# Softplus as one ScalarE function, expert ranks from comparisons and running sums, and a lead-in in another order

## The chip, the core and the metric

The kernel runs on one core of a Trainium2 chip. The time is the device time of one execution in microseconds, as the median of several runs. TensorE (PE) multiplies matrices, VectorE (DVE), ScalarE (ACT) and GpSimd (POOL) work elementwise on 128 partitions, and SyncE (SP) issues transfers.

## The reference, cut to what matters

Four batches of 1024 tokens with 256 features pass through four residual blocks: a selective state-space block, a mixture of 512 tiny experts beside a dense MLP, a linear attention, and the same mixture again. All arithmetic is fp32.

```python
# state-space block on the layer-normed x
conv  = conv_b + sum(xp[:, k:k+L, :] * conv_w[:, k] for k in range(4))
x     = silu(conv)                                   # 512 channels
delta = softplus(x @ wd1.T @ wd2.T + wd2_b)
A     = -exp(A_log)                                  # 512 x 16
h     = exp(delta*A) * h + (delta*x) * B_l           # per token, 16 states
y     = einsum('ben,bn->be', h, C_l) + x * W_D
out   = resid + (y * silu(skip)) @ out_w.T

# experts: two queries per token against 64 keys each
scores2, idx2 = top_k(routing, 8)                    # sx, sy and ix, iy
all_scores = sx[:, :, None] + sy[:, None, :]         # 64 pairs
all_idx    = ix[:, :, None] * 64 + iy[:, None, :]
scores, pk = top_k(all_scores, 8)
indices    = all_idx[pk]                             # beyond 511: the gather takes 511
ew  = silu(x @ down_embed[indices]) * softmax(scores)
out = ew @ up_embed[indices] + (silu(x @ gate_w) * (x @ up_w)) @ down_w
```

## The kernel before

The 4096 tokens are eight groups of 512; two groups are one sequence. Four stages follow one another.

**Scan.** For each group and each of the 16 states there is one step `s`, cut into two halves of two 128-channel tiles. In a half GpSimd multiplies `u = dx * bt` (`times_b`, L717; `bt` is a row of B, read back from DRAM to all partitions), ScalarE computes two decays `a = exp(delta * a_neg)` (`decay`, L731), DVE runs two recurrences `h` of 512 tokens, TensorE transposes the last step's `h`, and DVE adds it, times C, onto `acc` (`sum_up`). Beside this, work of other groups is woven in by generators: `prepare` makes the next group's projections, convolution, `delta` and `dx`; `finish` and `norm` end the last group; `mlp` is the dense MLP of earlier groups. Each `yield` in them names an estimated cost for TensorE and ScalarE, and `tick` (L640), called once per half step, decides by these costs which stages go out. A stage whose ScalarE cost exceeds `LONG = 4.0` is a lump: a table load, a function over 128x2048, and a load back for the decays. The engine orders come out pinned as written.

`softplus(z)` was built from pieces (`parts`, L362, to `chain`, L424): `e = |z|` and `delta = relu(z)` on ScalarE, `e = exp(-e)`, `dx = e + 1`, `delta += e` on GpSimd, `e = ln(dx)`, `dx -= 1`, `delta -= dx`, `delta += e`; then `dx = delta * xc`. In the first group (`alone`), DVE does the elementwise part.

**Lead-in** (L674 to L704). Ahead of the first step: GpSimd scales the identity into convolution taps `cds` and `w_d`, then `statistics(0)`, `prepare(0)`, the stores of `conv_d`, loads of x, and `a_neg`; `statistics(1)` comes at the first step (L769).

**Experts** (`experts`, L1155). For each group `route` (L977) makes a table `tb` of the weights of the 512 experts, per token: the top 8 of each query's 64 scores (`max`, `max_index`), the pairs' top 8, and with `iota`-comparisons a threshold `most` for each of the eight x-keys and a `rank` for each of the 64 y-keys; GpSimd multiplies out all 8 x 64 weights, and DVE sets those with a rank over the threshold to zero. A 128x2048 `eq` buffer serves both. `route` is a generator too, advanced one stage in each of eight steps per group. TensorE transposes `tb` into PSUM, which `apply` multiplies onto `wt`; the rest of the MLP queue runs beside it.

**Attention**, and then **ffn** (L1337), the last block: per group sixteen gate and up products, the experts, `route(g + 1)`, and `raise_x`.

Of the kernel before, what the change touches and what calls it, by code (L numbers as in the profile page):

```python
# [13 lines left out]
U32 = mybir.dt.uint32  # L14
# [6 lines left out]
P = 128  # L21
# [30 lines left out]
class Net:  # L52
# [59 lines left out]
    def ssm(self, xs, hs, behind):  # L112
# [6 lines left out]
        with ExitStack() as ctx:  # L119
# [22 lines left out]
            def load_x(g):  # L142
                xw_at[g] = now[0]
                xw[g] = late4.tile([P, TG, D], F32, tag="x", name="xw")
                sp.dma_start(out=xw[g], in_=xv[g])
# [7 lines left out]
            in_w0 = weights("in_wT")  # L153
            conv_w = self.load(wp, "conv_w", [P, EC, KC])
# [11 lines left out]
            ones = wp.tile([P, 1], F32, tag="ones", name="ones")  # L166
            dve.memset(ones, 1.0)
            mones = wp.tile([P, 1], F32, tag="mones", name="mones")
            dve.memset(mones, -1.0)
# [76 lines left out]
            def prepare(g, got, cds=None):  # L246
# [7 lines left out]
                def evac(out, ps, scale=None, bias=None):  # L254
                    if not alone:
# [100 lines left out]


                delta = two.tile([P, EC, G], F32, tag="delta", name="delta")
                dx = two.tile([P, EC, G], F32, tag="dx", name="dx")
                e = one.tile([P, EC, G], F32, tag="xe", name="e")  # L360

                def parts(c, ps):  # L362
                    b = wd2_b[:, c : c + 1]
                    act.activation(e[:, c, :], ps, AF.Abs, bias=b)
                    if alone:
                        dve.tensor_scalar(delta[:, c, :], ps, b, 0.0, ALU.add, ALU.max)
                    else:
                        act.activation(delta[:, c, :], ps, AF.Relu, bias=b)

                ps = z(0)  # L370
                for c in range(EC - 1):
                    yield 0.9, 1.2
                    parts(c, ps)
                    ps = z(c + 1)
                yield 3.4, 1.2
                parts(EC - 1, ps)
                ps = bank([2 * N, G], "bc")
                mul(ps, [(wbc[:, c, :], xc[:, c, :]) for c in range(EC)])
                yield 0, 1.9
                act.activation(e, e, AF.Exp, scale=-1.0)  # L380
                yield 0.3, 2.6
# [10 lines left out]

                if alone:
                    dve.tensor_scalar(dx, e, 1.0, None, ALU.add)
                else:
                    act.activation(dx, e, AF.Identity, bias=ones)

                def tt(out, a, b, op, c):
                    elem.tensor_tensor(out[:, c, :], a[:, c, :], b[:, c, :], op)

                tt(delta, delta, e, ALU.add, 0)
                tt(delta, delta, e, ALU.add, 1)
                yield 0, 4.7
                cT = late2.tile([P, TG, N], F32, tag="cT", name="cT")
                evac(cT, ps[:, :, N:])
                tt(delta, delta, e, ALU.add, 2)
                tt(delta, delta, e, ALU.add, 3)
                act.activation(e, dx, AF.Ln)
                yield 1.7, 2
                if alone:  # L410
                    dve.tensor_scalar(dx, dx, -1.0, None, ALU.add)
                else:
                    act.activation(dx, dx, AF.Identity, bias=mones)
# [10 lines left out]
                def chain(c):  # L424
                    tt(delta, delta, dx, ALU.subtract, c)
                    tt(delta, delta, e, ALU.add, c)
                    tt(dx, delta, xc, ALU.mult, c)

                if alone:
                    for c in range(EC):  # L430
                        chain(c)
                ps = w_skip(0)
                for t in range(1, TG):
                    yield 1.7, 1.3
                    evac(gate[:, t - 1, :], ps)
                    ps = w_skip(t)
                    if not alone:
                        chain(t - 1)
# [15 lines left out]
                yield 0.9, 1.3  # L454
                evac(gate[:, TG - 1, :], ps)
                gates[g] = gate
                if not alone:
                    chain(TG - 1)
# [215 lines left out]
            with ExitStack() as lead:  # L674
                tp = lead.enter_context(tc.tile_pool(name="ssm_lead", bufs=1))
                cds = {}
                for c in range(EC):
                    cds[c] = tp.tile([P, KC, P], F32, tag=f"cd{c}", name=f"cd{c}")
                    for k in range(KC):
                        pool.tensor_scalar(  # L680
                            cds[c][:, k, :], self.ident, conv_w[:, c, k : k + 1], 1.0,
                            ALU.mult, ALU.mult,
                        )
                for c in range(EC):
                    pool.tensor_scalar(
                        w_d[:, c, :], self.ident, w_d_col[:, c : c + 1], 1.0,
                        ALU.mult, ALU.mult,
                    )
                for _ in statistics(0):
                    pass  # L690
                for _ in prepare(0, data[0], cds):
                    pass
                for c in range(EC):
                    sp.dma_start(out=conv_d[c], in_=cds[c])
                for g in range(1, 4):
                    load_x(g)
                act.activation(a_neg, a_log, AF.Exp)
                dve.tensor_scalar(a_neg, a_neg, -1.0, None, ALU.mult)
            thr = scan.enter_context(
                tc.tile_pool(name="ssm_thr", bufs=2, reuse_waits="tile")  # L700
            )
            four = scan.enter_context(
                tc.tile_pool(name="ssm_four", bufs=4, reuse_waits="tile")
            )  # L704
# [52 lines left out]
            for q in range(AHEAD):  # L757
                times_b(q)
            before, kept_state, stats, begun = None, None, iter(()), {0, 1}
            for s in range(NG * N):  # L760
                g, n = s // N, s % N
                first = g % 2 == 0
                if n == 0 and g + 1 < NG:
# [5 lines left out]
                    if g == 0:  # L769
                        for _ in statistics(1):  # L770
                            pass
# [177 lines left out]
    def expert_weights(self, pool):  # L949
        nc, w, eng = self.nc, {}, self.nc.sync  # L950
        w["W_q"] = self.load_rows(pool, "W_q", KD, 2 * NKEY, eng)

        w["keys"] = []
        for t in range(2):
            kb = pool.tile([P, 2, NKEY], F32, tag=f"keys{t}", name=f"keys{t}")
            nc.gpsimd.memset(kb, 0.0)
            for i in range(2):
                eng.dma_start(out=kb[i * 64 : (i + 1) * 64, i, :], in_=self.io["keys"][t])
            w["keys"].append(kb.rearrange("p a b -> p (a b)"))

        w["iota"] = pool.tile([P, NKEY], F32, tag="iota", name="iota")
        nc.gpsimd.iota(
            w["iota"], pattern=[[1, NKEY]], base=0, channel_multiplier=0,
            allow_small_or_imprecise_dtypes=True,
        )
        w["iota32"] = pool.tile([P, NKEY], F32, tag="iota32", name="iota32")
        nc.vector.tensor_scalar(w["iota32"], w["iota"], 32.0, None, ALU.mult)
        w["steps"] = pool.tile([P, TOPK], F32, tag="steps", name="steps")
        nc.vector.tensor_scalar(w["steps"], w["iota"][:, 0:TOPK], 1.0, None, ALU.add)
# [7 lines left out]
    def route(self, nc, w, g, qT, pools, got):  # L977
# [7 lines left out]
        M4 = 4  # L985
# [10 lines left out]
        r = sm.tile([P, 2 * M4, NKEY], F32, tag="r", name="r")  # L996
        nc.scalar.copy(r, ps.rearrange("p t m (h k) -> p (t m h) k", h=2))
        yield
        v = sm.tile([P, 2 * M4, TOPK], F32, tag="v", name="v")
        iu = sm.tile([P, 2 * M4, TOPK], U32, tag="iu", name="iu")  # L1000
        for i in range(2 * M4):
            if i == M4:
                yield
            nc.vector.max(v[:, i, :], r[:, i, :])
            nc.vector.max_index(iu[:, i, :], v[:, i, :], r[:, i, :])
        yield
        fi = sm.tile([P, 2 * M4, TOPK], F32, tag="fi", name="fi")
        nc.vector.tensor_copy(fi, iu)
        fx, fy = fi[:, 0:M4, :], fi[:, M4:, :]
# [3 lines left out]
        nc.vector.tensor_tensor(  # L1013
            d[:, :, :NKEY], r, top.to_broadcast([P, 2 * M4, NKEY]), ALU.subtract
        )
        nc.vector.tensor_tensor(
# [14 lines left out]

        pv, left, pw = pairs("pv"), pairs("left"), pairs("pw")
        nc.vector.tensor_tensor(
            grid(pv), over(v[:, 0:M4, :], 3), over(v[:, M4:, :], 2), ALU.add
        )
        sc = sm.tile([P, M4, TOPK], F32, tag="sc", name="sc")
        for i in range(M4):
            nc.vector.max(sc[:, i, :], pv[:, i, :])
            nc.vector.match_replace(left[:, i, :], sc[:, i, :], pv[:, i, :], -3.0e38)
        yield  # L1040
        nc.vector.tensor_tensor(left, left, pv, ALU.not_equal)
        cnt = sm.tile([P, M4, TOPK], F32, tag="cnt", name="cnt")
        nc.vector.tensor_reduce(cnt, grid(left), AX.X, ALU.add)

        nc.vector.tensor_tensor(
            grid(pw), over(d[:, 0:M4, NKEY:], 3), over(d[:, M4:, NKEY:], 2), ALU.mult
        )
        nc.vector.tensor_tensor(pw, pw, left, ALU.mult)
        zi = sm.tile([P, M4], F32, tag="zi", name="zi")
        nc.vector.tensor_reduce(zi, pw, AX.X, ALU.add)  # L1050
        nc.vector.reciprocal(zi, zi)

        f64 = sm.tile([P, M4, TOPK], F32, tag="f64", name="f64")
        nc.vector.tensor_scalar(f64, fx, float(NKEY), None, ALU.mult)
        nc.vector.tensor_tensor(grid(pv), over(f64, 3), over(fy, 2), ALU.add)
        nc.vector.scalar_tensor_tensor(
            pv, pv, float(NEXP - 1), pw, ALU.is_ge, ALU.mult
        )
        last = sm.tile([P, M4], F32, tag="last", name="last")
        nc.vector.tensor_reduce(last, pv, AX.X, ALU.add)  # L1060
        nc.vector.tensor_tensor(last, last, zi, ALU.mult)
        yield

        nc.vector.tensor_tensor(
            grid(pw), w["iota"][:, 0:TOPK].unsqueeze(1).unsqueeze(3).to_broadcast(sh),
            over(fx, 2), ALU.is_equal,
        )
# [389 lines left out]
```

## Time and profile before

| | |
|---|---|
| time, median of 3 runs | 2168.31 us (2165.47 to 2179.81) |
| the profiled execution | 2167.88 us, its span 2166.2 |
| granted TensorE clock | 0.955 |
| busy: TensorE, VectorE, ScalarE, GpSimd | 1914.2, 1592.9, 1019.4, 1032.6 us |
| chain that ended last, by engine | PE 57%, DVE 22%, ACT 12%, issue 5%, POOL 3%, DMA 2% |
| first recurrence, its second pair | 83.57 us, 91.10 us |
| scan, experts, attention, ffn | to about 1197, 1460, 1690, 2166 us |

Busy time is summed over the whole span; what bounds a stage is read from that stage. The chain that ended last is followed back from the last instruction, at each step to what released it. In a line for a group of instructions stand its line, engine and operation, output and inputs, shapes, count; then busy us and mean ns of one; then the engine's idle time just before. In a line for one tile, the three durations are minimum, median and maximum in ns.

### The profile page before, as it was taken

The page shows a single profiled execution, that of the slowest core. Times are in us where ns is not written, and L with a number is a line of the kernel's source. Part 1 is how long each engine was busy: PE and PEld are TensorE (multiplying, and loading weights), DVE is VectorE, ACT ScalarE, POOL GpSimd, SP SyncE. Part 2 cuts the span into 40 slices and gives each one's busy share as a digit, 9 for nine tenths or more (in the row PEclk, how much of TensorE's full clock was granted, in tenths as well). Part 3 has the DMA queues.
Part 4 walks back from the last instruction along what each step waited for, and adds up shares of the span by engine and source line. Part 5 has one row for each costly group of instructions (what it writes and reads, how often), then busy time and mean ns, then how long its engine had stood idle before and what let it go on. Part 6 is the DMA issues. An engine that isn't in the chain of part 4 may idle for free.

```text
span 2166.2 us, 22802 instructions
## 1 busy us (share of the span) xinstructions
PE 1914.2 (88%) x7712; PEld 1209.5 (56%) x7712; DVE 1592.9 (74%) x2843; ACT 1019.4 (47%) x1557; POOL 1032.6 (48%) x691
## 2 busy tenths in 40 slices
PE   6585888988979989899888889969998999999999
PEld 2334545655645655556464555646665456666665
DVE  2798998978989979888798789984446545555551
ACT  2366676767766777677656233213332311111111
POOL 2569779687787886877886223311111000000000
PEclk9798999999999999999999999989999999999999
DMA  2311212122122221221212222120000000000000
GB/s 74 98 54 27 81 49 76 51 79 76 52 83 73 72 73 52 76 81 50 73 40 88 98 77 89 49 83 1 1 1 1 1 10 10 10 10 10 10 10 10
DMA packets 84757, 106.13 MB, mean 49 GB/s; under 512 B 7840, under 2 KB 53920, under 8 KB 84640
## 3 DMA queue, kind: packets, MB, share of 16 engines
q1 hardware_dynamic: 78064, 98.00, 14.6%
q10 hardware_dynamic: 6576, 6.67, 1.0%
q8 instruction: 61, 1.00, 0.2%
q14 instruction: 56, 0.46, 0.1%
HBM read 90.75 MB, written 13.89 MB: 48 GB/s over the span
## 4 chain that ended last, share of the span: by engine, by line
PE 57%; DVE 22%; ACT 12%; issue 5%; POOL 3%; DMA 2%; ACTq 0%; SPq 0%; DVEq 0%; POOLq 0%
PE ps L106 23%; PE hT L47 5%; PE gate L47 4%; DVE h L47 4%; PE conv L47 4%; DVE acc L47 4%; PE up L47 3%; ACT L47 3%; ACT a L47 3%; PE xin L47 2%; PE dt L47 2%; PE out L47 2%; PE down L47 2%; DVE eq L47 1%; ACT av L47 1%
## 5 line engine op out<-in xcount | busy, mean ns | idle before, releaser
L47 POOL TENSOR_TENSOR u<-dx,bt 128x1024 f32<-128x1024 f32 x256 | 604.1, 2368 | 264.0 <-DVE h L47 137.0
L47 PE MATMUL hT<-ident,h 128*128 128x128 f32 x2048 | 305.7, 290 | 120.4 <-DVE acc L47 118.2
L47 DVE SCALAR_TENSOR_TENSOR acc<-hT,cT,acc 128x512 f32<-128x512 f32 x512 | 355.9, 736 | 40.3 <-PE hT L47 39.3
L47 PEld LDWEIGHTS hT<-ident,h 128*128 128x128 f32 x2048 | 247.2, 148 | 245.1 <-DVE acc L47 194.4
L47 ACT ACTIVATE a<-delta,a_neg 128x512 f32<-128x512 f32 x512 | 340.1, 688 | 92.1 <-DVE h L47 72.2
L47 DVE TENSOR_TENSOR_SCAN h<-a,state,u 128x512 f32<-128x512 f32 x256 | 314.9, 1267 | 38.7 <-ACT a L47 37.6
L47 DVE TENSOR_TENSOR_SCAN h<-a,u 128x512 f32<-128x512 f32 x256 | 299.4, 1206 | 59.2 <-ACT a L47 52.0
L1079 POOL TENSOR_TENSOR tb<-ex,d 128x2048 f32<-128x2048 f32 x8 | 29.2, 3644 | 400.7 <-PE ps L106 330.7
L1379 DVE TENSOR_TENSOR act<-s,ps 128x512 f32<-128x512 f32 x64 | 43.8, 685 | 145.2 <-PE ps L106 145.1
L1377 ACT ACTIVATE s<-ps 128x512 f32<-128x512 f32 x64 | 38.2, 597 | 230.1 <-PE ps L106 222.2
L47 ACT ACT_TABLE_LOAD x92 | 118.0, 1283 | 56.6 <-DVE d L47 33.9
L47 PE MATMUL gate<-hT,gate_w 128*128 128x512 f32 x256 | 124.2, 618 | 8.2 <-DMA gate_w<-in_gate_w 8.2
L47 PE MATMUL up<-hT,up_w 128*128 128x512 f32 x256 | 124.0, 610 | 7.5 <-ACT a L47 6.3
L47 PE MATMUL down<-w_down_w,av 128*128 128x256 f32 x512 | 121.0, 382 | 7.9 <-DVE xw L47 7.9
L106 PE MATMUL ps<-hT,w_gate_w 128*128 128x512 f32 x256 | 121.9, 599 | 4.4 <-DVE act L1379 4.4
L106 PE MATMUL ps<-hT,w_up_w 128*128 128x512 f32 x256 | 120.3, 592 | 0.0
L106 PE MATMUL ps<-w_down_w,act 128*128 128x256 f32 x512 | 116.6, 380 | 3.9 <-DVE x L1151 3.9
L47 PEld LDWEIGHTS down<-w_down_w,av 128*128 128x128 f32 x512 | 95.5, 191 | 29.4 <-issue 9.3
L106 PEld LDWEIGHTS ps<-w_down_w,act 128*128 128x128 f32 x512 | 96.0, 190 | 22.1 <-DVE x L1151 9.7
L47 PE MATMUL conv<-xin,taps 128*128 128x512 f32 x224 | 104.8, 595 | 1.5 <-ACT xc L47 1.5
L47 POOL TENSOR_TENSOR tb<-ex,d 128x2048 f32<-128x2048 f32 x8 | 43.8, 5478 | 117.6 <-DVE code L47 117.6
L47 POOL TENSOR_TENSOR av<-av,up_v 128x512 f32<-128x512 f32 x64 | 87.7, 1374 | 12.0 <-ACT up_v L47 12.0
(250 smaller groups left out, 3275.7 us busy)
## 6 DMA issues: line engine op xcount, KB each, us to landing
bt<-bcd SPq DMA_DIRECT2D x128, 256.0 KB, 3.3
gate_w<-in_gate_w SPq DMA_DIRECT2D x64, 128.0 KB, 3.0
up_w<-in_up_w SPq DMA_DIRECT2D x64, 128.0 KB, 2.4
hT<-hs SPq DMA_DIRECT2D x16, 512.0 KB, 4.3
taps<-conv_d SPq DMA_DIRECT2D x28, 256.0 KB, 3.8
xw<-in_x SPq DMA_DIRECT2D x8, 512.0 KB, 4.3
in_wT<-in_in_wT SPq DMA_DIRECT2D x8, 512.0 KB, 4.6
skip_wT<-in_skip_wT SPq DMA_DIRECT2D x8, 512.0 KB, 4.6
```

What stands on the lines that cost most here:

```text
L47: return self.tc.keep_in_program_order(f(*args, **kw))
L106: self.nc.tensor.matmul(ps, lhsT=lhsT, rhs=rhs, start=i == 0, stop=i == len(pairs) - 1)
L1079: nc.gpsimd.tensor_tensor(tbv, ex.unsqueeze(3).to_broadcast(sht), d[:, M4:, 0:NKEY].unsqueeze(2).to_broadcast(sht), ALU.mult,)
L1377: nc.scalar.activation(s, pg, AF.Silu)
L1379: nc.vector.tensor_tensor(a, s, pu, ALU.mult)
```

## The change

Three parts change.

Softplus becomes one function of ScalarE. In the first group it reads PSUM directly, 128x512 at a time; in the others the bias is added in the evacuation and one 128x2048 function follows. GpSimd keeps only `dx = delta * xc` (in the first group DVE does three of four). The stages have other costs, one fewer is there, and so `tick` deals out the others differently: the MLP's `down` products and lumps come in other half steps.

In the route, the positions of maxima are no longer asked for. `match_replace` marks the top 8, a comparison with all keys and a sum count the values above each key, a running sum over powers of 8 counts, among equal ones, those ahead of it, and the result is a rank for each key. `ex` and GpSimd's product come before this part. The route has two stages more.

The lead-in is ordered anew: x(0) comes in four transfers, x(1) behind `in_wT`; `a_neg` is first; `statistics(0)` is ahead of the taps, `statistics(1)` inside `prepare(0)`; later evacuations of group 0 are ScalarE's; `conv_d`, later x, `W_q` and the keys go out behind the first row of B.

```diff
 def evac(out, ps, scale=None, bias=None):
-    if not alone:
+    if not alone or g in bcds:
...
-def parts(c, ps):
+def step_sizes(c, ps):
     b = wd2_b[:, c : c + 1]
-    act.activation(e[:, c, :], ps, AF.Abs, bias=b)
     if alone:
-        dve.tensor_scalar(delta[:, c, :], ps, b, 0.0, ALU.add, ALU.max)
+        act.activation(delta[:, c, :], ps, AF.Softplus, bias=b)
+        by_x(c)
     else:
-        act.activation(delta[:, c, :], ps, AF.Relu, bias=b)
+        evac(delta[:, c, :], ps, bias=b)
+
+def by_x(c):
+    eng = dve if alone and c < EC - 1 else pool
+    eng.tensor_tensor(dx[:, c, :], delta[:, c, :], xc[:, c, :], ALU.mult)
...
-yield 0, 1.9
-act.activation(e, e, AF.Exp, scale=-1.0)
-yield 0.3, 2.6
+yield 0.3, 5.1
...
-    act.activation(dx, e, AF.Identity, bias=ones)
-tt(delta, delta, e, ALU.add, 0)
...
-act.activation(e, dx, AF.Ln)
...
-    act.activation(dx, dx, AF.Identity, bias=mones)
+if not alone:
+    act.activation(delta, delta, AF.Softplus)
+yield 0, 0.6
...
-def chain(c):
-    tt(delta, delta, dx, ALU.subtract, c)
-    tt(delta, delta, e, ALU.add, c)
-    tt(dx, delta, xc, ALU.mult, c)
...
+thr = scan.enter_context(tc.tile_pool(name="ssm_thr", bufs=2))
+four = scan.enter_context(tc.tile_pool(name="ssm_four", bufs=4))
+act.activation(a_neg, a_log, AF.Exp)
+dve.tensor_scalar(a_neg, a_neg, -1.0, None, ALU.mult)
+for _ in statistics(0):
+    pass
...
+for i, _ in enumerate(prepare(0, data[0], cds)):
+    if i == 8:
+        for _ in statistics(1):
+            pass
...
 row(0)
-for q in range(AHEAD):
+times_b(0)
+for c in range(EC):
+    sp.dma_start(out=conv_d[c], in_=cds[c])
+for g in range(2, 4):
+    load_x(g)
+for out, src in self.asked:
+    sp.dma_start(out=out, in_=src)
+for q in range(1, AHEAD):
     times_b(q)
```

The route, and the two places that call it:

```diff
-    nc.vector.max_index(iu[:, i, :], v[:, i, :], r[:, i, :])
+    dve.match_replace(
+        kept[:, i % M4, at], v[:, i, :], r[:, i, : at.stop - at.start], LOW
+    )
...
+def ranks(name):
+    return one.tile([P, M4, NR], F32, tag=name, name=name)
+
+def eights(name):
+    return sm.tile([P, M4, TOPK], F32, tag=name, name=name)
...
+eq = one.tile([P, M4, NR, TOPK], F32, tag="eq", name="eq")
+for t, at in enumerate((slice(0, TOPK), slice(TOPK, NR))):
+    of, n = slice(t * M4, (t + 1) * M4), at.stop - at.start
+    dve.tensor_tensor(
+        eq[:, :, at, :], v[:, of, :].unsqueeze(2).to_broadcast([P, M4, n, TOPK]),
+        r[:, of, :n].unsqueeze(3).to_broadcast([P, M4, n, TOPK]), ALU.is_gt,
+    )
+yield
+above = ranks("above")
+dve.tensor_reduce(
+    above.rearrange("p m j -> p (m j)"),
+    eq.rearrange("p m j b -> p (m j) b"), AX.X, ALU.add,
+)
+free = eq.rearrange("p m j b -> p (m j b)")
+def part(i, n=M4 * NR):
+    return free[:, i * NEXP : i * NEXP + n].rearrange("p (m j) -> p m j", m=M4)
+unit, per, step = part(0), part(1), 3.0 * 2**23
+for x, by in ((unit, step), (per, -step)):
+    dve.tensor_scalar(
+        x.bitcast(I32), above, by, 127.0 * 2**23, ALU.mult, ALU.add
+    )
+yield
+digits = free[:, 2 * NEXP : 2 * NEXP + 1 + M4 * NR]
+dve.memset(digits[:, 0:1], 0.0)
+dve.scalar_tensor_tensor(
+    digits[:, 1:].rearrange("p (m j) -> p m j", m=M4), kept, LOW, unit,
+    ALU.is_equal, ALU.mult,
+)
+rank = ranks("rank")
+dve.tensor_tensor_scan(
+    rank.rearrange("p m j -> p (m j)"), digits[:, : M4 * NR],
+    w["follows"].rearrange("p m j -> p (m j)"), 0.0, ALU.add, ALU.mult,
+)
+dve.tensor_tensor(rank, rank, per, ALU.mult)
+dve.tensor_scalar(per, rank, -3.5, 1.5 * 2**26, ALU.add, ALU.add)
+dve.scalar_tensor_tensor(rank, per, 1.5 * 2**26, rank, ALU.subtract, ALU.subtract)
+dve.tensor_tensor(rank, above, rank, ALU.subtract)
+dve.tensor_scalar(kept, kept, LOW, 8.0, ALU.not_equal, ALU.mult)
+dve.tensor_tensor(rank, rank, kept, ALU.add)
...
-    eqv, rank.unsqueeze(2).to_broadcast(sht),
-    most.unsqueeze(3).to_broadcast(sht), ALU.is_le,
+    eqv, rank[:, :, TOPK:].unsqueeze(2).to_broadcast(sht),
+    most.unsqueeze(3).to_broadcast(sht), ALU.is_lt,
 )
 dve.tensor_tensor(tbv, tbv, eqv, ALU.mult)
...
 begin(0)
+next(routes[0])
 next(routes[0])
...
-                    if k == 6:
+                    if k > 5:
                         next(routes[g + 1])
```

## The prediction, made before the changed kernel ran

> **What bounds the kernel now.** I read the table of stretches first, cut where the stages change. Columns: stretch and length, then busy us (and instructions) of TensorE, its weight loads, VectorE, ScalarE and GpSimd, then clock, DMA share, GB/s.
>
> ```profile
> core 0: us, PE busy (x) PEld busy (x) DVE busy (x) ACT busy (x) POOL busy (x), PEclk, DMA share, GB/s
> 589.00:732.00 143.00, 127.88 (x573) 82.72 (x572) 123.31 (x153) 102.66 (x158) 115.62 (x77) 0.98 0.23 71
> 1195.00:1460.00 265.00, 230.78 (x881) 153.91 (x881) 228.79 (x635) 71.45 (x101) 72.53 (x32) 0.94 0.24 79
> 1690.00:2166.00 476.00, 463.49 (x1586) 285.85 (x1584) 238.06 (x599) 86.78 (x126) 29.15 (x8) 1.00 0.03 9
> ```
>
> In one scan group PE (128 of 143) and DVE (123) are both near full and neither is alone the bound. In the expert stage both are at 86-87%; from 1320 to 1420 DVE is busy 19.1 to 19.9 of every 20 us. The last stage is TensorE's (97%). Attention (1460 to 1690) isn't touched.
>
> Then the chain that ended last, at the start: start, length, work.
>
> ```profile
> 16.67 0.42 DVE rn L47
> ...
> 53.42 0.68 DVE bc L47
> 54.10 1.13 DVE dx L47
> ...
> 57.85 1.28 ACT L47
> 59.15 1.92 ACT e L47
> ...
> 72.68 0.61 DVE gate L47
> ...
> 81.41 0.10 DVE a_neg L47
> ...
> 88.35 2.08 ACT rn L47 x4
> 90.42 0.58 ACT a L47
> ...
> 91.10 2.35 DVE h L47 x2
> ```
>
> From 54.1 to 72.7 DVE writes softplus out by itself, with ScalarE's Ln in the middle; then group 1's statistics hold up the recurrence (its second pair of steps starts at 91.10). Last, groups of instructions, and waits between 588 and 1018 us (three groups):
>
> ```profile
> L47 POOL TENSOR_TENSOR delta<-delta,e 128x512 f32<-128x512 f32 x56 | 70.6, 1273 | 2.2
> L47 ACT ACTIVATE dx<-e,ones 128x2048 f32<-128x2048 f32 x7 | 14.0, 1999 | 0.0
> DVE h L47 <- ACT a L47: 37.0, 17, 4.0
> ACT e L47 <- POOL delta L47: 5.1, 3, 1.8
> ```
>
> The recurrence waits for ScalarE 12 us per group, mostly behind lumps of 4.5 us: a table load, a 128x2048 function of 1.9, a load back.
>
> **Lead-in.** A_log's negative exponential now stands ahead of the first statistics on DVE. Its transfer was issued at 4.31 and took 5.9 us, and its issue on ScalarE's queue comes later now, since SyncE's queue carries four pieces of x ahead; behind the waiting DVE multiply stand BN stats, GpSimd's 4.8 us of statistics and everything else. I put rn at 19.1 instead of 16.67: +2.4. Then TensorE's 36.7 us as before, bc copy at 55.9. Softplus is four ScalarE functions of 0.69 straight from the z banks, beside z's matmuls (3.9 us), with one load; dx is three DVE multiplies of 0.69 and one of GpSimd's. So the 18.6 us of DVE arithmetic leave the path; the skip products (sixteen of .5, 8.2) end at 64.6, x times W_D and its last copy (3.6 + .6) at 68.8, table load and first decay at 70.8. Gate and acc copies go to ScalarE, .6 each beside those matmuls. GpSimd's first u, behind the bt row, is due about 66. Statistics of group 1 lie inside TensorE's convolution. ScalarE does rn of group 1 (2.1) ahead of the second decays, so the second pair starts near 74.1 instead of 91.10: **-17**, or -10 if the bt row is late (on SyncE's queue only the skip weights and x(1) are near it), -20 if A_log arrives in time. Behind the first bt rows SyncE now issues conv_d's four stores (3.25 us before, at 54.58), two x, W_q and keys, eleven in all, some 8 us at that spacing; the third row waits for that, but is used two steps, 14 us, after the first. Cost 0; without that cover 8. The two pools that lose an argument for their waits have the same waits at each u in the instruction lists: 0.
>
> **Softplus in seven groups.** Removed per group: ScalarE four Relu copies (.6 issue spacing), one exponential 1.9, two Identity passes 2.0: 8.3 us; GpSimd twelve operations of 1.27: 15.3 us. Softplus takes Ln's place, one 128x2048 instruction. TensorE's and DVE's work per group is unchanged, so the engines' sums don't shrink where it counts. I added, over the 32 half steps of one group, the larger of TensorE's and DVE's work: 134.8 us before, 134.6 after, against 143.3 measured. Only the 8.5 us of stalls can go. Half steps run at 3.5 us where nothing intervenes; the ones at 23, 27, 29, 30 and 0 of group 4 took 6.2, 6.1, 6.4, 6.1 and 7.8. Of these the table lumps stay (their count is the same, 116 table loads in the program, 115 after); what goes is Ln's wait for GpSimd (1.7), GpSimd's late dx (about 2.5 at half 27), and the exponential (1.5 at half 20): some 4 of 8.5 per group, while gate lumps now meet at halves 27 and 30. Group by group: -5 in the first (there the recurrence also waited for GpSimd's u 4.3 us and dx 2.5), then -3, -7 for two, -8 for two, -3, -4: **-30**. Nothing gained would be 0, all stalls gone -60.
>
> Here a rule speaks against the change: the Trainium skill, "ScalarE: Activation LUTs", Rules for kernel authors, says exp and ln come from one table set, one load for both, and What ACT_TABLE_LOAD costs prices a switch at 2.66 us, drain included. By that, before would switch nothing for Ln, and Softplus would add two switches a group, 2 x 2.66 x 8 = +43. The row says otherwise: a load stands before Ln (57.85) and another after it, and Ln starts at 59.15, straight after 1.28 us, with no drain. So I take 0 for switches. That Softplus takes a 2048-wide function's time, 1.9 us, no row shows; Ln, Exp and Silu all have it here. At twice that, +1.9 in each of 7 lumps, +13; less than Ln's time I exclude, since no function here has it.
>
> **Ranks in the expert stage.** Per route FIND_INDEX8 (218 ns) becomes MATCH_REPLACE8 (209): even. Out go the 256-element index sums and comparison, in come a 256-element comparison, a reduction 288 wide over 2304 (+.3) and some fourteen operations on 288 or 32 elements. Laid out at DVE's spacing (.33 us for independent 256-element work, .46 where each waits for the last, as here), a route goes from 21.9 to about 26.5: +4.6, eight times = 37. Two of the eight stretches between routes have DVE idle 13.0 and 5.9 us, which hides 9. What DVE delays here is TensorE's transposes of the table: late table, idle TensorE.
>
> The large comparison follows ex directly, the very moment GpSimd starts its table product from ex:
>
> ```profile
> L47 DVE TENSOR_TENSOR eq<-iota,code x8: 2291/2292/5580, 1227.6 to 1435.0; 128x2048 f32<-128x2048 f32 x8
> L1107 DVE TENSOR_TENSOR eq<-rank,most x8: 4497/4718/4726, 1702.8 to 2098.2; 128x2048 f32<-128x2048 f32 x8
> L47 POOL TENSOR_TENSOR tb<-ex,d x8: 3620/5736/5765, 1227.6 to 1435.0; 128x2048 f32<-128x2048 f32 x8
> ```
>
> One of eight was second and took 5.58 instead of 2.29. "SBUF — State Buffer", SBUF: two separate sides, calls this an exclusive lock: the later fully blocks. The price of losing is then 3.3 us, of winning 0. DVE now issues two comparisons, so GpSimd may slip in between; I take it to lose two in eight, +3 in all: **+30** (+15 with more slack, +66 if it always loses).
>
> **Last stage.** Eight routes grow 3.2 us each, under TensorE's 58.8 us a group, where DVE is half idle. x adds are due 18.2 us into a group and end at 14 to 17, so all but some tenths are hidden: **+1.5** (-4 to +6). Without that cover it would be +26.
>
> **Sum.** -17 - 30 + 30 + 1.5 = -15.5 on the profiled execution, 2167.9 (span 2166.2 and 1.7 around it), which stands .4 below the median 2168.3, a difference I leave out: **2152**.
>
> **The rivals.** *More relief in the scan:* taking GpSimd from 116 to 100 us and ScalarE from 103 to 94 frees u and decays everywhere; GpSimd's u waits 51 us for the recurrence in three groups, which speaks against its being late, the 12 us per group of waiting for decays for it. All stalls gone: -30 more, 2122. *No relief:* the lumps are the stalls and stay; the scan gives 0: 2182. *Ranking on a full engine, the slower side:* in the DVE-bound stage each route pays 4.9 of dependent operations and 3.3 for the lost port, 8.2 x 8 = 66, with no slack: -17 - 30 + 66 + 1.5 = +20, **2188**. It decides from 5.7 us a route, (17 + 30 - 1.5)/8. Speaking for it is the full DVE from 1320 to 1420; against it, seven of eight comparisons that went first. *That Softplus isn't one instruction* is excluded: the instruction list has one per tile.
>
> **How the numbers follow.** The case as summed 0.45 (its own range 2135 to 2170), more relief 0.25, no relief 0.15, ranking 0.15. A measurement here tells 1% from no change: 2146.6 and 2190. Faster: most of more relief, .23, and the lower third of the first, .15: 0.38. Slower: two thirds of ranking and the tail of no relief, 0.13. The rest 0.49. The range reaches to both outer cases: 2118 to 2188.
>
> **What would show it.** Second recurrence pair near 74 (lead-in; at 80 or later, A_log or bt is what waits). Groups of about 139 us, with ScalarE's functions no longer waiting for GpSimd. Expert stage 295, the comparison at 2.29 in most routes. The last stage 477. The forecast is wrong if Softplus takes longer than 1.9 us, or if the stalls left by GpSimd are taken by other lumps.

## The result, and the profile after

The changed kernel takes 2202.2 us (median of 4 runs, 2201.7 to 2204.2) against 2168.6 before: 1.0147 times as long, with an interval of 1.0111 to 1.0184. The forecast was 2152, with a range to 2188. It is slower, past even the rival that had placed the loss in the ranking. Of the runs of the kernel before that were timed beside the experiments, those with a granted clock of 0.953 or more took 2162 to 2170 us, and those with 0.951 or less 2173 to 2180.

Where the time went, by stage of the two profiled executions (the scan is counted from the second pair of recurrences):

| stage | before | after | difference | forecast |
|---|---|---|---|---|
| lead-in, to the second pair | 91.1 | 72.7 | -18.4 | -17 |
| scan | 1105.5 | 1110.7 | +5.2 | -30 |
| experts | 262.3 | 312.0 | +49.7 | +30 |
| attention | 208.6 | 206.2 | -2.4 | 0 |
| last stage | 498.7 | 498.7 | 0.0 | +1.5 |
| span | 2166.2 | 2200.3 | +34.1 | -15.5 |

The stages are cut here where their work changes, so attention ends earlier than in the prediction's stretches (at 1667.5 in the kernel before). The table of stretches for the changed kernel: one scan group, the expert stage, the last stage. Then the expert stage of the kernel before, cut at its own ends.

```profile
619.95:764.96 145.01, 129.68 (x572) 84.13 (x571) 121.97 (x153) 96.32 (x155) 101.17 (x65) 0.95 0.22 70
1183.40:1495.40 312.00, 239.97 (x872) 159.31 (x872) 281.72 (x723) 70.77 (x99) 56.91 (x31) 0.88 0.19 64
1701.60:2200.30 498.70, 482.62 (x1670) 296.65 (x1668) 287.75 (x729) 96.77 (x142) 31.53 (x11) 1.00 0.03 9
```

```profile
1196.60:1458.90 262.30, 229.51 (x872) 153.11 (x872) 226.50 (x632) 70.53 (x99) 71.45 (x31) 0.93 0.24 78
```

In the scan GpSimd is down from 116 to 101 and ScalarE from 103 to 96, as costed, and yet the group takes 145. In the expert stage VectorE has 55.2 us more work and the stage is 49.7 longer. TensorE runs the same 872 products at a granted clock of 0.88 instead of 0.93, ten microseconds slower. Attention's -2.4 is clock as well: in its last part TensorE does the same products at 0.86 instead of 0.81 (18.6 us for 21.0). In the last stage VectorE has 38 us more work under TensorE's 483, and nothing shows.

The chain that ended last, at the start of the changed kernel:

```profile
4.83 6.63 DMA w_A_log<-in_A_log
...
11.97 0.34 DVE st L47
...
18.84 0.43 DVE rn L47
...
54.92 0.69 DVE bc L47
...
72.70 2.35 DVE h L47 x2
```

The first normalised tile was forecast for 19.1, the bc copy for 55.9, the second pair for 74.1. From 55.7 on TensorE works without a gap to 66.8; no elementwise softplus is left in the chain.

The answer for the tile `eq`, of the changed kernel (count, then minimum, median and maximum in ns; both comparisons together), then the groups of instructions for the long comparison in the expert stage and for GpSimd's product:

```profile
L47 DVE TENSOR_TENSOR eq<-v,r x16: 418/2149/5709, 1211.1 to 1460.9; 128x256 f32<-128x256 f32 x8, 128x2048 f32<-128x2048 f32 x8
```

```profile
L47 DVE TENSOR_TENSOR eq<-v,r 128x2048 f32<-128x2048 f32 x8 | 42.2, 5279 | 0.0
L47 POOL TENSOR_TENSOR tb<-ex,d 128x2048 f32<-128x2048 f32 x8 | 29.2, 3645 | 160.6 <-DVE ex L47 140.5
```

GpSimd's product now takes 3.6 us in every route, where it was 5.74 in most, and VectorE's long comparison takes 5.71 in seven of eight, where it was 2.29 in seven of eight. In the eighth the long one takes 2.28, but the short one ahead of it 2.02 instead of 0.42. The price has changed sides.

### The profile page after: what moved, and what is told of

The parts are those of the page before. It is cut to its first block, busy times and chain, and to the rows that moved or that the text cites. A ratio compares the mean times of both kernels' runs of the same rounds, so it can differ in the third digit from the quotient of the medians.

```text
span 2200.3 us, 22820 instructions
## 1 busy us (share of the span) xinstructions
PE 1924.0 (87%) x7712; PEld 1223.1 (56%) x7712; DVE 1665.0 (76%) x2991; ACT 969.7 (44%) x1514; POOL 914.5 (42%) x608
## 4 chain that ended last, share of the span: by engine, by line
PE 59%; DVE 24%; ACT 9%; issue 5%; POOL 2%; DMA 1%; ACTq 0%; SPq 0%; DVEq 0%
PE ps L106 22%; PE hT L47 7%; PE conv L47 4%; PE gate L47 4%; DVE acc L47 4%; DVE h L47 3%; PE down L47 3%; PE up L47 3%; ACT L47 3%; DVE eq L47 3%; PE skip L47 2%; ACT a L47 2%; PE xin L47 2%; PE out L47 2%; PE dt L47 2%
## 5 line engine op out<-in xcount | busy, mean ns | idle before, releaser
L47 PE MATMUL hT<-ident,h 128*128 128x128 f32 x2048 | 311.3, 295 | 136.6 <-DVE acc L47 134.2
L47 PEld LDWEIGHTS hT<-ident,h 128*128 128x128 f32 x2048 | 253.8, 151 | 245.6 <-DVE acc L47 197.1
L1044 POOL TENSOR_TENSOR tb<-ex,d 128x2048 f32<-128x2048 f32 x8 | 29.0, 3620 | 400.4 <-DVE ex L1037 400.4
L47 POOL TENSOR_TENSOR tb<-ex,d 128x2048 f32<-128x2048 f32 x8 | 29.2, 3645 | 160.6 <-DVE ex L47 140.5
```

Of the source, the lines that this page charges most:

```text
L47: return self.tc.keep_in_program_order(f(*args, **kw))
L1044: nc.gpsimd.tensor_tensor(tbv, ex.unsqueeze(3).to_broadcast(sht), d[:, M4:, 0:NKEY].unsqueeze(2).to_broadcast(sht), ALU.mult,)
```

## The experiments

Two theories stood against each other for each of the two stages that missed. Experts: the port that VectorE and GpSimd share, or the added operations. Scan: Softplus brings relief that another order of work gives back, or there was no relief to be had. Ratios are to runs of the kernel before that were made beside each experiment (medians 2167.6, 2169.0 and 2168.3); differences in us are to the changed kernel's 2202.2.

**The route alone, in the kernel before.**

```diff
 # before.py, with route, its constants and its calls from after.py
-    nc.vector.max_index(iu[:, i, :], v[:, i, :], r[:, i, :])
+    dve.match_replace(
+        kept[:, i % M4, at], v[:, i, :], r[:, i, : at.stop - at.start], LOW
+    )
...
```

> The kernel before with the new route alone (Softplus, scan and lead-in as before). If the whole loss is the route's, the expert stage goes from 262 to about 310 and the time to 2168 + 48 = 2216; if the scan's new order also hands a backlog of MLP work to the expert stage, less than +35 comes from the route, at most 2203.

Measured: 2222.7 (2214.8 to 2231.2), ratio 1.0251 (1.0204 to 1.0297). The expert stage takes 311.2, as in the changed kernel: the route is the whole of that loss. Another +10.8 is in the scan of the profiled execution, whose instructions are those of the kernel before; its granted clock was 0.94 to 0.95 in groups 3 to 5 instead of 0.97 to 0.98, which is taken up at the end.

**The two comparisons swapped.**

```diff
-for t, at in enumerate((slice(0, TOPK), slice(TOPK, NR))):
+for t, at in ((1, slice(TOPK, NR)), (0, slice(0, TOPK))):
```

> The changed kernel, with the comparison over 64 keys issued ahead of the one over the eight kept values. Theory (GpSimd's table product wins the port because the short comparison fills just the 0.35 us in which GpSimd wakes up): now the long comparison starts right behind ex and goes first, 2.29 us instead of 5.71 in seven of eight routes of the expert stage, GpSimd's product stretches from 3.6 to about 5.7, which nobody waits for; -24 us, 2178. Rival (the port doesn't set the end, the chain of small operations does, or GpSimd still goes first): within 4 us of 2202.

Measured: 2203.6 (2201.2 to 2209.1); the expert stage is 312.0 again. The rival's number, but not its reason. VectorE's and GpSimd's rows around one route, first of the changed kernel, then with the swap (start, length, idle time before):

```profile
1279.43 0.19 DVE L47 TENSOR_TENSOR ex<-d,zi 128x32 f32<-128x32 f32 x1
1279.54 6.04 DVE L47 TENSOR_TENSOR eq<-v,r 128x256 f32<-128x256 f32 x2
1279.79 3.65 POOL L47 TENSOR_TENSOR tb<-ex,d 128x2048 f32<-128x2048 f32 x1 [20.10 <-DVE ex L47]
```

```profile
1278.42 0.19 DVE L47 TENSOR_TENSOR ex<-d,zi 128x32 f32<-128x32 f32 x1
1278.53 6.04 DVE L47 TENSOR_TENSOR eq<-v,r 128x2048 f32<-128x2048 f32 x2
1278.78 5.51 POOL L47 TENSOR_TENSOR tb<-ex,d 128x2048 f32<-128x2048 f32 x1 [20.10 <-DVE ex L47]
```

GpSimd starts 0.36 us after ex has started. In the changed kernel the short comparison (0.42) fills that time, and the long one finds the port taken. With the swap the long one goes first (2.28) and GpSimd waits, but then GpSimd gets the port and the short one takes 3.84 instead of 0.42. The pair costs 6.04 both times. So it doesn't help to change which of the two is second.

**The short comparison ahead of ex.**

```diff
+compare(0, slice(0, TOPK))
 ex = eights("ex")
...
-for t, at in enumerate((slice(0, TOPK), slice(TOPK, NR))):
-    of, n = slice(t * M4, (t + 1) * M4), at.stop - at.start
...
+compare(1, slice(TOPK, NR))
 yield
```

> The changed kernel with the comparison of the eight kept values issued ahead of ex, so that only the long one follows ex and only one-input work follows that. Theory (whichever two-input operation of DVE meets GpSimd's table product pays for it): the long comparison takes 2.29 in all eight routes, no other takes over the wait, DVE loses 24 us of work and the expert stage about nine tenths of that: 2202 - 22 = 2180. Rival (the expert stage isn't set by DVE's two comparisons; some other operation is blocked in their place): as with the swapped comparisons, within 4 us of 2202.

Measured: 2190.1 (2186.6 to 2192.3), ratio 1.0087 (1.0053 to 1.0121): -12, half of the forecast.

```profile
L47 DVE TENSOR_TENSOR eq<-v,r x16: 393/1339/3883, 1212.5 to 1450.6; 128x256 f32<-128x256 f32 x8, 128x2048 f32<-128x2048 f32 x8
...
L47 POOL TENSOR_TENSOR tb<-ex,d x8: 3621/5510/5512, 1213.2 to 1450.9; 128x2048 f32<-128x2048 f32 x8
...
L47 DVE TENSOR_TENSOR tb<-tb,eq x8: 2285/2292/3256, 1228.0 to 1466.9; 128x2048 f32<-128x2048 f32 x8
```

The long comparison takes 2.28 to 2.29 in seven routes and GpSimd waits again (5.51); in the second route statistics stand behind ex, and it takes 3.88. VectorE has 258.5 us of work instead of 281.7, and the stage is 15.2 shorter: two thirds of what VectorE lost, not nine tenths. So the mechanism is shown, and its size was put too high. TensorE's waits in the expert stage show which part is gone: the table's transposes `st` wait for `tb`, the experts' output products `o` for VectorE's adds onto `x` (us in total, times, longest). First the changed kernel, then this one:

```profile
PE st L47 <- DVE tb L47: 32.8, 7, 8.1
PE o L47 <- DVE x L47: 14.7, 6, 5.7
```

```profile
PE st L47 <- DVE tb L47: 32.4, 7, 8.1
PE o L47 <- DVE x L47: 2.4, 2, 1.4
```

With the port no longer lost, the wait for `x` falls by 12.3. The wait for the table stays (3.2 in the kernel before): in the next experiment, without the running sums, it falls to 6.0, while the wait for `x` stays at 15.6. So each cause shows mainly in a wait of its own.

**Without the running sums.**

```diff
-digits = free[:, 2 * NEXP : 2 * NEXP + 1 + M4 * NR]
...
-dve.tensor_tensor(rank, rank, kept, ALU.add)
+rank = above
```

> The changed kernel without the running sum that orders equal scores: the rank is the count of values above alone, so ten operations on 288 elements per route are left out (equal keys would share a rank). Theory (DVE is full in the expert stage): about 4.4 us for each of eight routes, -35 us, 2167; the last stage unchanged. Rival (only the port's loss counts, the small operations lie in DVE's idle time): -10 or less, above 2192.

Measured: 2171.5 (2167.6 to 2173.6), 31 below the changed kernel, near the theory's 35 and far from the rival's 10, and level with the kernel before (1.0004, 0.9989 to 1.0018). The expert stage falls from 312.0 to 280.7, VectorE's work in it by 33.9, the last stage by 2. In the expert stage the running sums cost twice what the lost port does (31.3 and 15.2).

**The old stage costs.**

```diff
-yield 0.3, 5.1
+yield 0, 1.9
+yield 0.3, 2.6
 bc = one.tile([2 * N, G], F32, tag="db", name="bc")
...
-if not alone:
-    act.activation(delta, delta, AF.Softplus)
-yield 0, 0.6
+yield 0, 4.7
 cT = late2.tile([P, TG, N], F32, tag="cT", name="cT")
 evac(cT, ps[:, :, N:])
+if not alone:
+    act.activation(delta, delta, AF.Softplus)
-yield 1.7, 0
+yield 1.7, 2
...
```

> The changed kernel with the kernel before's stage costs and number of stages in prepare (one stage is empty), so that TensorE's order in groups 1 to 7 is again that of the kernel before, half step by half step, while Softplus, the lead-in and the route stay. Theory A (Softplus does relieve the scan, the new dealing of MLP work to the last half steps gave it back): groups of about 139 us instead of 145, 2202 - 35 = 2167. Theory B (the removed ScalarE and GpSimd work was never what the scan waited for): groups as before the change, 142 to 143 us, 2202 minus 5 to 12 = 2190 to 2197.

Measured: 2189.6 (2188.2 to 2194.9), -12.6: just past theory B's lower edge, and the scan alone fell by 13.0 (1110.7 to 1097.7). The 4312 matrix products up to the end of the scan follow one another in the same order in the kernel before, in the one with the route alone and here. The half steps of groups 2 to 6 (counted from 0), as means, from the starts of the recurrences (us):

```
half steps   before   route alone   old costs   changed
0              6.3        6.3          6.7        4.5
1-2            7.2        7.2          7.2        7.2
3-4            7.2        7.2          7.2        9.6
5-9           22.1       22.4         22.3       19.4
10-13         16.1       16.1         16.1       17.4
14-18         21.6       21.6         21.6       21.7
19             3.9        5.2          5.2        3.9
20             5.0        5.1          5.1        4.0
21-22          8.0        8.0          8.0       11.3
23             6.1        6.1          4.1        3.6
24-26         12.5       12.5         12.5       11.6
27-31         27.1       27.6         27.3       30.7
all          143.0      145.1        143.2      145.1
```

With TensorE's order unchanged (third column beside the first two), Softplus moves one half step: 23, by 2.0, where Ln had waited for GpSimd. That is real relief, 2 us per group. Half steps 20 and 27, where I had put the exponential and the late dx, stay as they were. For the second, the recurrence that ends half step 27 of group 4, before and with the old costs:

```profile
760.39 2.34 DVE L47 TENSOR_TENSOR_SCAN h<-a,u 128x512 f32<-128x512 f32 x2 [2.51 <-POOL dx L47]
```

```profile
733.03 2.34 DVE L47 TENSOR_TENSOR_SCAN h<-a,u 128x512 f32<-128x512 f32 x2 [2.30 <-ACT a L47]
```

Before, two things ended within 0.1 us of each other: GpSimd's dx (at 760.32) and the first decay, which stands behind a copy of TensorE's `gate` products on ScalarE. With dx out of the way, the wait for the decay is nearly as long. The changed order (last column beside the third) gains 2.9 at 5-9 and 0.9 at 24-26, and loses 2.4 at 3-4, 1.3 at 10-13, 0.5 at 19-23 and 1.2 at 27-31 with 0: no single place. I put it down to MLP products that now meet other work, and only one place was followed up, half step 30, where the second Silu lump of the group has a pile of products behind it. The chain of the changed kernel there (the half step begins at 750.1):

```profile
750.48 0.59 ACT av L47
...
751.09 1.28 ACT L47
...
752.38 1.91 ACT av L47
...
754.31 1.28 ACT L47
...
755.61 0.70 ACT a L47
...
757.47 0.74 DVE acc L47
...
758.25 1.97 PE hT L47 x8
760.22 5.39 PE up L47 x8
```

TensorE stands behind the lump, then does eight `up` products in one half step, which takes 8.7 us (5.8 as a mean before).

**Both, and the running sums out as well.**

```diff
 # the first: the short comparison ahead of ex, and the old stage costs
 # the second: these, no running sums, and
-dve.tensor_scalar(a_neg, a_neg, -1.0, None, ALU.mult)
 for _ in statistics(0):
     pass
+dve.tensor_scalar(a_neg, a_neg, -1.0, None, ALU.mult)
```

> The same, with the kernel before's stage costs in prepare as well. Theory: the two gains lie in different stages and add up: 2202 - 22 - 13 = 2167, level with the kernel before. Rival (MLP work that the scan finishes earlier or later comes back in the expert stage): more than 2175.

> The same without the running sums (equal keys would share a rank), and with the multiply of a_neg behind the first statistics on DVE. Theory: the route then costs DVE less than in the kernel before, the expert stage is back at 260 to 264 and the lead-in's and first group's gain stays: 2202 - 49 - 13 - 2 = 2138. Rival: TensorE binds the expert stage before DVE does, so part of it is lost: 2150.

Measured: 2172.3 (2168.7 to 2178.1), ratio 1.0006 (0.9990 to 1.0022), between the two numbers: the gains add up and more, since 30 is 5 over the 12.1 and 12.6 that each edit gives alone; no run shows where these 5 come from. And 2130.8 (2125.7 to 2137.8), ratio 0.9813 (0.9764 to 0.9862), 7 below the theory; the lead-in, which gave 6.5 instead of 2, is most of that. The expert stage is 263.5 there, with VectorE busy 226.0: the numbers of the kernel before.

**a_neg later, alone.**

> The changed kernel with the multiply of a_neg behind the first statistics on DVE, so that these don't wait for A_log's transfer. If that wait sets the first statistics, the first normalised tile starts at 16 to 17 instead of 18.84 and the second pair of recurrences at about 70.5 instead of 72.7, the time falls by 2; if x's four pieces arrive as late, nothing moves.

Measured: 2196.5 (2 runs within 0.2), -5.8. The normalised tile starts at 11.12 and the second pair at 66.1, 6.6 earlier. The first piece of x is there at 3.0 us; the statistics begin then. So the multiply had cost almost three times the 2.4 that the prediction gave it.

**What gained, with the running sums kept.**

```diff
-dve.tensor_scalar(kept, kept, LOW, 8.0, ALU.not_equal, ALU.mult)
-dve.tensor_tensor(rank, rank, kept, ALU.add)
```

> A version that keeps the running sums, put together from what gained: the comparison of eight ahead of ex, the kernel before's stage costs, a_neg's multiply behind the first statistics; and the two operations that add 8 to the ranks of keys outside the top 8 are left out, since such a key already has eight values above it, or values above and equals ahead of it that make eight. Theory (DVE's chain of operations sets the expert stage at nine tenths of its length): 2172 - 5.5 - 8 x 0.76 x 0.9 = 2161, 0.996 of the kernel before. Rival (the operations that remain leave TensorE waiting for the tables as before): 2167, no difference.

Measured: 2163.5 (2155.8 to 2168.0, 22 runs), ratio 0.9960 (0.9946 to 0.9975): between the two numbers, nearer to the theory, and a version ahead of both kernels, by a little. The two operations took 5.7 from the expert stage (295.8 to 290.1), as forecast; it is still 28 over that of the kernel before.

## Why the prediction was wrong, point by point

The profiled execution missed its sum by 49.6 us (+34.1 for -15.5): 35.2 in the scan, 19.7 in the expert stage, and -5.3 in the other three.

**Lead-in: right**, -18.4 for -17, and its milestones each within 2.1 us. Two terms were mis-sized in a way that the sum doesn't show. The first tile came 2.2 later than before (I said 2.4), but without the wait for A_log it comes 5.6 earlier (11.12 against 16.67), as x comes in pieces and the statistics no longer stand behind the taps on GpSimd, where they waited for W_D's transfer until 10.4. So the wait costs 7.7 at the first tile, and "-20 if A_log arrives in time" would have been -25.

**Expert stage: the mechanism was right, one term mis-sized.** The step that failed is "I take it to lose two in eight, +3 in all". The long comparison lost seven in eight: (5.71 - 2.29) x 7, less the one of 3.3 before, is 20.6, and the short one lost 1.6 in the eighth route. Of the 55.2 us of VectorE's added work that leaves 33.0 for the added operations, 4.1 a route for the forecast 4.6. I had read off the row that seven of eight comparisons went first and called it a race. The trace of before had the answer, in the one that lost:

```profile
1403.67 0.18 DVE L47 TENSOR_TENSOR ex<-d,zi 128x32 f32<-128x32 f32 x1
1403.77 0.18 DVE L47 SCALAR_TENSOR_TENSOR code<-fi,steps 128x32 f32<-128x32 f32 x1
1403.87 0.42 DVE L82 BATCH_NORM_STATS2 bnst<-x 128x6 f32<-128x256 f32 x1
1404.02 3.62 POOL L47 TENSOR_TENSOR tb<-ex,d 128x2048 f32<-128x2048 f32 x1 [16.36 <-DVE code L47]
1404.20 5.58 DVE L47 TENSOR_TENSOR eq<-iota,code 128x2048 f32<-128x2048 f32 x1
```

GpSimd starts 0.33 to 0.36 us after the start of ex, in all eight routes of the expert stage and in each kernel. Here an operation of 0.42 stood between and the comparison came too late; where only shorter ones did (at 1257.02 ex, at 1257.33 the comparison, at 1257.37 GpSimd) it came first. The change puts 0.42 us of other work there in seven routes. And of VectorE's added work the stage hid 5.5, not 9.

**Scan: wrong, and by more.** -30 became +5.2. The first group gave -5.7 for -5. In the other seven, -25 was to come from three kinds of stall. Ln's wait for GpSimd went (2.0 a group, forecast 1.7). The step that failed is the other two, "GpSimd's late dx (about 2.5 at half 27), and the exponential (1.5 at half 20)": half step 20 is filled by TensorE's eight `bc` products (3.6 us) and stays at 5.0 to 5.1, and 27 stays at 5.3 to 5.4; in group 4 the decay there was as late as dx. A stall near an operation that goes is not yet that operation's stall. And the new order, which I named ("gate lumps now meet at halves 27 and 30") and gave no price, took back what was left: old stage costs alone give 12.6. With the old ScalarE costs for the evacuations alone, the instruction lists are those of the changed kernel, so these costs don't change the order; what remains is how the stages around Softplus are cut and priced. Which of the moved products cost what stays open but for half step 30.

**Table switches and Softplus's time: right.** The program loads tables once less (115 for 116), and Softplus takes what Ln took. First Ln before, then Softplus after (count, then busy us, mean ns of one, idle before it):

```profile
L47 ACT ACTIVATE e<-dx 128x2048 f32<-128x2048 f32 x8 | 15.3, 1912 | 13.5 <-POOL delta L47 13.5
```

```profile
L47 ACT ACTIVATE delta<-delta 128x2048 f32<-128x2048 f32 x7 | 13.4, 1914 | 0.1
```

The two more switches a group that the prediction weighed (+43) are not there.

**Last stage: right**, 0.0 for 1.5. VectorE's work grew by 4.8 a route there, not 3.2, and all of it was hidden.

**The rival** "ranking on a full engine" was the one to believe: 8.2 a route was forecast under it, VectorE's work grew by 6.9, and the stage by 6.2, over the 5.7 from which it decides. Its number, 2188, still held the scan's -30.

## What to carry to other kernels

When two engines share a port, ask what the first of them runs in the few tenths of a microsecond that the other takes to wake up, and what comes second; a long two-operand instruction directly at the release goes first, and behind it belongs work that keeps its time beside the other engine (here statistics at 0.39 us and a reduction at 2.54; one TENSOR_SCALAR took 1.37 instead of 0.30 beside another product of GpSimd). When a planner deals out work by named costs, removing work changes where everything else lands, so price the new order half step by half step. And the wait list names only what ended last: before counting a stall as gone with its operation, look at what ends just ahead of it.

## What the hardware showed that was not expected

TensorE's clock answered to the same short gap differently in two executions. In half step 19 of group 4 TensorE waits 1.92 us for `xw`, in the kernel before and in the one with only the route changed, and then does the same eight products:

```profile
718.64 1.99 PE L47 MATMUL down<-w_down_w,av 128*128 128x256 f32 x8 [1.92 <-DVE xw L47]
```

```profile
722.13 3.12 PE L47 MATMUL down<-w_down_w,av 128*128 128x256 f32 x8 [1.92 <-DVE xw L47]
```

The granted clock over the 9.0 and 9.5 us around them is 1.00 in the first and 0.89 in the second. The half step takes 3.9 and 5.5 us, the scan 1105.5 and 1116.3, in the executions that were profiled. The Trainium skill ("TensorE: Matmul & The Clock Gate", What's actually happening) tells of an activity window of 3.4 us that runs freely, so that the same kernel meets it at different points; a gap of 1.9 is shorter than that, and what else decides it no run here shows. It also means that the scan's +5.2 and the -13.0 with the old costs, each from one execution, can carry some microseconds of clock. In the five executions with the changed order a group of 2 to 6 took 145.1 us each time, in the two with Ln 143.0 and 145.1, in the four with Softplus in the old order 142.8 to 143.9. The 2.0 of half step 23 is free of this: it takes 6.1 in both executions with Ln, and 4.1 in all four with Softplus in that order.
